# A sandwich of attention and routed experts on one core: the experts' matrices first copied into another layout in memory

## The chip, the cores and the metric

The kernel runs on one core of a Trainium2 chip. The metric is device time in microseconds, from the start of the program to its end; of several executions the median counts. The core has a matrix engine (PE, with its weight loads shown as PEld), a vector engine (DVE), a scalar engine (ACT), GpSimd (POOL) and a synchronisation engine (SP) that here issues transfers. ACT and POOL issue transfers too. All transfers are carried by the core's 16 DMA engines. Everything is float32 but for a few small masks.

## The reference

The input is x, 8 sequences of 512 rows of 256 numbers. Cut to what matters, the reference computes:

```python
x = x + layernorm(attention(layernorm(x)))     # 16 heads of 128 in 4 groups, causal, sinusoidal positions
x = x + layernorm(ffn(layernorm(x)))

def ffn(x):                                    # 4096 rows
    scores = softmax(x @ gate_w.T)             # 64 experts
    topk_w, topk_idx = top_k(scores, 6)
    # an expert takes the first 64 rows (CAP) that chose it, in the order of rows
    d = (silu(buf @ w_gate) * (buf @ w_up)) @ w_down   # per expert: 64 x 256, 256 x 176 twice, 176 x 256
    y = sum over the 6 choices of topk_w * d
    return y + (silu(x @ sh_gate.T) * (x @ sh_up.T)) @ sh_down.T     # shared expert, width 352
```

Every expert has three matrices: w_gate and w_up of 256 x 176 and w_down of 176 x 256, 180 KB each. The kernel takes the 64 experts two at a time, as 32 pairs; a pair's matrices are 1.08 MB.

## The kernel before, in words

The eight sequences are worked through one after the other, and each as 16 heads, so that one loop runs over 128 heads k. The order of the instructions on each engine is the order in which the program writes them: the whole loop stands under a manual schedule.

One step of the loop does parts of several heads. It writes the scores of head k in four row tiles (PE), adds the causal mask and finds each row's extreme (DVE, line 293), and takes the exponential (ACT, line 296). `weigh` (line 300) divides by the row sums: a reciprocal on DVE and four multiplications on POOL (line 306). The weights of head k - 1 must be turned before they can be multiplied with the values. `turned` (line 313) does this in two halves: DVE turns 32 x 32 blocks into the tile eb (line 322), SP writes eb to a memory tensor ex_d (line 326), waits for it, and reads it back in four transfers with the blocks at their new places, as et (line 329). `mix` of head k - 2 (line 343) multiplies et with the values on PE (pav, line 349), and ACT copies the result to ao (line 109). `project` of head k - 3 multiplies ao with the output matrix (po, line 361). So the exchange through memory that starts in one step is needed by PE in the next step.

Beside the heads stands other work, hung into the steps by tables: the keys and values of the next sequence, and for a sequence that is done its normalisation, its shared expert and its routing. After five sequences (EARLY) the rows of the experts are settled but for places left free. From head 94 on `experts` (line 621) is advanced at several places of each step: first tables, then the 32 pairs. Once it runs in full, a head's step advances it four times, which is two pairs.

A pair m passes through stages (lines 628 to 642). At its step m POOL gathers its 128 rows (gx, line 513). One step later ACT issues the loads of its gate and up matrices, `load_gate_up` (line 517): two transfers into the tile wgu, each with 2 x 128 rows of 1408 bytes, since a partition holds two neighbouring rows of an expert's matrix, and the two experts lie apart in memory. Two steps later PE turns the gathered rows (ptx), a step after that it multiplies them with gate and up (pgu, line 549), and ACT issues `load_down` (line 526): one transfer into wd, 2 x 88 rows of 2048 bytes. Then the hidden rows are turned (pth), and five steps after the gather PE multiplies them with wd (pd, line 575); ACT scales the result (dd, line 583), and POOL adds it into the memory tensor y_d by an indirect transfer (line 586). The tiles wgu and wd have two buffers each, so a load waits until PE is done with the pair two before it.

One more pair, "late", takes rows of the last three sequences. It is chosen at run time; its loads are issued by SP (table["m"] is a register), at head 102. A loop at the end would take further such pairs; it runs no turns here.

Transfers issued by SP and by ACT take eight completion semaphores in turn: each waits, on its issuing engine, for the transfer eight before it in the program's order. A transfer that waits holds up what stands behind it on that engine; on ACT these are exponentials and copies.

The memory tensors are tiles of a pool, made by dram.tile at the start of the kernel.

Of the kernel before, what the change touches and what calls it, by code (L numbers as in the profile page):

```python
# [11 lines left out]
F32 = mybir.dt.float32  # L12
# [7 lines left out]
P = 128  # L20
B, T, E = 8, 512, 256
# [7 lines left out]
NH = G * QPG  # L29
NX, F, TOPK, CAP = 64, 176, 6, 64  # L30
FC = F // 2
NM = NX // 2
# [12 lines left out]
def sandwich_kernel(ctx, tc, x, wq, bq_t, wkv, bk_t, bv, wo, gate_wt, w_gate, w_up, w_down,  # L45
                    sh_gate_t, sh_up_t, sh_down_t, pe_t, out):
    nc = tc.nc
# [3 lines left out]
    dram = ctx.enter_context(tc.tile_pool(name="dram", bufs=1, space=bass.MemoryType.DRAM))  # L51
# [10 lines left out]
    x1_d = dram.tile([NT, E], F32, tag="x1_d", name="x1_d")  # L62
    xg_d = dram.tile([ET_ROWS + 1, ROW], F32, tag="xg_d", name="xg_d")
    y_d = dram.tile([2 * (ET_ROWS + CAP), E], F32, tag="y_d", name="y_d")
    lxg_d = dram.tile([NT - ET_ROWS, LROW], F32, tag="lxg_d", name="lxg_d")
    ly_d = dram.tile([NT - ET_ROWS, E], F32, tag="ly_d", name="ly_d")

# [55 lines left out]
    with ExitStack() as part:  # L123
# [38 lines left out]
        for half, (t, w) in enumerate(((sg_sb, sh_gate_t), (su_sb, sh_up_t))):  # L162
            nc.sync.dma_start(out=t[:, :, :FSH], in_=w.rearrange("(c p) n -> p c n", p=P))
            nc.sync.dma_start(out=t[:, :, FSH:],
                              in_=gate_wt.rearrange("(c p) n -> p c n", p=P)[:, :, ts(half, NX // 2)])
# [39 lines left out]
        def zeros():  # L205
            zero = p1.tile([P, ROW], F32, tag="hid", name="zero")
            nc.gpsimd.memset(zero, 0.0)
            nc.sync.dma_start(out=xg_d[ET_ROWS : ET_ROWS + 1, :], in_=zero[0:1, :])
            nc.sync.dma_start(out=y_d[ET_ROWS : ET_ROWS + CAP, :], in_=zero[:CAP, :E])
            yield  # L210
            for r in range(ET_ROWS + CAP, 2 * (ET_ROWS + CAP), P):
                n = min(P, 2 * (ET_ROWS + CAP) - r)
                nc.sync.dma_start(out=y_d[r : r + n, :], in_=zero[:n, :E])
                yield
# [85 lines left out]
        def weigh(k):  # L300
            l = live[k]
            recip = small.tile([P, NI], F32, tag="recip", name=f"recip_{k}")
            nc.vector.reciprocal(recip, l["total"])  # L303
            engine = nc.gpsimd if k < NK - 1 else nc.vector
            for n, e in enumerate(l["e"]):
                engine.tensor_scalar(e, e, recip[:, n : n + 1], 1.0, ALU.mult, ALU.mult)  # L306
# [200 lines left out]
        table, pairs = {}, {}  # L507

        def start_pair(m):

            l = pairs[m] = {"m": m}
            l["gx"] = p3.tile([P, ROW], F32, tag="gx", name=f"gx_{m}", bufs=3)
            nc.gpsimd.indirect_dma_start(
                out=l["gx"], out_offset=None, in_=xg_d[:, :],
                in_offset=bass.IndirectOffsetOnAxis(ap=table["idx"][:, m, 0:1], axis=0))

        def load_gate_up(key):
            l, queue = pairs[key], nc.sync if key == "late" else nc.scalar
            m = l["m"]

            l["wgu"] = p3.tile([P, 2, 2, 2, F], F32, name=f"wgu_{key}", **l.get("wgu_at", {"tag": "wgu"}))
            for k, w in enumerate((w_gate, w_up)):
                queue.dma_start(out=l["wgu"][:, :, k, :, :].rearrange("p e c f -> p e (c f)"),
                                in_=w[ds(m * 2, 2)].rearrange("e (p c) f -> p e (c f)", p=P))

        def load_down(key):
            l, queue = pairs[key], nc.sync if key == "late" else nc.scalar
            m = l["m"]
            l["wd"] = p3.tile([FC, 2, 2, E], F32, name=f"wd_{key}", **l.get("wd_at", {"tag": "wd"}))
            queue.dma_start(out=l["wd"].rearrange("p e c h -> p e (c h)"),  # L530
                            in_=w_down[ds(m * 2, 2)].rearrange("e (p c) h -> p e (c h)", p=FC))

        def turn_rows(key):
            l = pairs[key]
            pt = ps_s.tile([P, 2, P], F32, tag="s", name=f"ptx_{key}")
            rows = l["gx"][:, :E].rearrange("s (p c) -> s c p", c=2)
            for c in range(2):
                nc.tensor.transpose(pt[:, c, :], rows[:, c, :], ident)
            l["gxt"] = p3.tile([P, 2, P], F32, tag="gxt", name=f"gxt_{key}")
            on_dve(l["gxt"], pt)  # L540
            l["gw"] = p3.tile([P, 2], F32, tag="gw", name=f"gw_{key}", bufs=4)
            nc.vector.tensor_copy(l["gw"], l["gx"][:, E + 2 * key : E + 2 * key + 2])
# [78 lines left out]
        def experts():  # L621


            yield from tables()
            yield
            yield from free_slots()
            yield
            for m in range(NM + 5):
                if m < NM:
                    start_pair(m)  # L630
                for behind_, step in ((5, down), (3, gate_up), (4, turn_hidden), (2, turn_rows),
                                      (1, load_gate_up), (3, load_down)):
                    if 0 <= m - behind_ < NM:
                        step(m - behind_)
                yield
                if 0 <= m - 3 < NM:
                    gate_up_hidden(m - 3)
                if 0 <= m - 5 < NM:
                    scatter(m - 5)
                if m == NM + 4:  # L640
                    pairs["all"] = True
                yield
# [288 lines left out]
        queries(0)  # L931
        assert len(units) == 12
        behind, ahead = {}, iter(())
        routed, zeroing = experts(), zeros()
        twice, finishing = False, False
        FIRST_FREE = (EARLY + 1) * NH + 6

        def side(s, place):
            behind.pop(f"{s}{place}", lambda: None)()
            if not b:  # L940
                for u in rest.get(f"{s}{place}", ()):
                    u()

        for k in range(NK):
            b, s = divmod(k, NH)
            active = k >= EARLY * NH + 14
            scores(k, 0)
            scores(k, 1)
            if 0 <= k - 1 < NK - 2:
                turned(k - 1)  # L950
            if twice and not finishing:
                next(routed, None)
            scores(k, 2)
            scores(k, 3)
            if k == NK - 1:
                turned_at_once(k - 1)
            weigh(k)
            side(s, "A")
            if k >= 3:
                project(k - 3)  # L960
            side(s, "B")
            if active:
                next(routed, None)
            if s == (9 if b == EARLY + 1 else 8):
                next(ahead, lambda: None)()
            if k + 1 < NK:
                queries(k + 1)
            side(s, "M")
            if k >= 2:
                mix(k - 2)  # L970
            if active and not finishing:
                next(routed, None)
            if not b:
                next(zeroing, None)
                next(zeroing, None)
            if k == FIRST_FREE:

                work = table["work"]
                table["rest"] = nc.values_load(work[0:1, 0:1], min_val=0, max_val=NM - 1)
                table["m"] = nc.values_load(work[0:1, 1:2], (ET.DVE, ET.SP), min_val=0, max_val=NM - 1)  # L980
                pairs["late"] = {"m": table["m"], "wgu_at": {"tag": "wgu_late", "bufs": 1},
                                 "wd_at": {"tag": "wd_late", "bufs": 1}}
                load_gate_up("late")
                load_down("late")
            if s == 2 and b:
                behind = feed_forward(b - 1)
            side(s, "D")
            if s == 6 and b + 1 < B:
                ahead = prepare(b + 1)

            for _ in range((0, 0, 0, 0, 0, 0, 1, 0, 1, 1, 2, 1, 1, 1, 2, 1)[s] if b == EARLY + 1 else
                           (0, 0, 0, 0, 0, 0, 1, 1, 1, 1, 1, 1, 1, 1, 2, 1)[s]):
                next(ahead, lambda: None)()
            twice = active and k > EARLY * NH + NH
            if twice and not finishing:
                next(routed, None)

            if finishing and s in (12, 14):
                next(routed, None)
            if active and not finishing and "all" in pairs:  # L1000
                routed, finishing = finish_early(), True
# [11 lines left out]
        with tc.For_i(0, table["rest"], 1) as n:  # L1013
            m = nc.values_load(table["work"][0:1, ds(n + 2, 1)], (ET.DVE, ET.SP), min_val=0, max_val=NM - 1)
# [4 lines left out]
            for b in range(EARLY, B):  # L1019
                q, tag = [(p1, "hid"), (p2, "v"), (p2, "v")][b - EARLY]  # L1020
                xg = q.tile([P, NI, LROW], F32, tag=tag, name=f"rest_xg_{b}")
                nc.sync.dma_start(out=xg, in_=rows_of(lxg_d, b * T - ET_ROWS))
                q, tag = [(p1, "y"), (p2, "x"), (p2, "x")][b - EARLY]
# [68 lines left out]
```

## Time and profile before

Three runs took 1455.51, 1459.09 and 1459.84 us; the median is 1459.09 us.

| | |
|---|---|
| profiled execution, its own time | 1456.37 us |
| its span | 1454.6 us |
| PE busy | 1403.1 us, 96% |
| DVE, ACT, POOL busy | 892.8, 505.8, 429.2 us |
| moved by DMA | 252.03 MB in 160790 packets, mean 173 GB/s |
| ACT's queue (q10) | 28672 packets, 39.85 MB, 9.9% of 16 engines' span |
| SP's queue (q1) | 125869 packets, 201.52 MB, 46.5% |
| loads of wgu, first and last issue | 980.8 and 1247.2 us |
| loads of wd, first and last issue | 995.5 and 1260.5 us |

The page gives one execution, taken by the hardware profiler. An engine's busy time is the sum of its instructions; what it spends on issuing transfers is not counted as busy. The page shows the span in 40 equal slices of 36.4 us, where a digit is a busy share in tenths, and PEclk is the granted clock of PE in tenths of full speed. In a list of waits, "A <- B: 8.3, 4, 4.3" says that A stood idle until B for 8.3 us in all, 4 times, 4.3 at the longest. In a list in order of time, each line has start, duration, engine, line of the program, operation, and in brackets the idle time before it and what ended it. A transfer is shown at its issue; where its data landed is seen in the packet records of the trace.

### The profile page before, as it was taken

Reading aid. Unit: us, or ns where it says so; the run is one execution under the profiler, and the core shown is the slowest. Engines: PE = TensorE matmul, PEld = TensorE weight load, DVE = VectorE, ACT = ScalarE, POOL = GpSimd, SP = SyncE. Lnnn points to the kernel's source line nnn. Section 1 sums busy time; section 2 is a strip of 40 time slices with the busy share of each in tenths; the row PEclk is TensorE's granted clock in tenths of the full one; section 3 lists DMA queues with packets and bytes.
Section 4 is the critical chain, followed back from the end, with each engine's and each line's share of the span. In section 5 each row is a group of like instructions: output and inputs, shape, how many; then the busy total and the mean of one; then the engine's idle time right before and its main releaser. Section 6 shows DMA issues by size and latency. Waiting matters only on the chain. (4 is left out here: it accounts for less than half of the span.)

```text
span 1454.6 us, 18553 instructions
## 1 busy us (share of the span) xinstructions
PE 1403.1 (96%) x5310; PEld 855.2 (59%) x5310; DVE 892.8 (61%) x3097; ACT 505.8 (35%) x1442; POOL 429.2 (30%) x686
## 2 busy tenths in 40 slices
PE   9999999999999999999999999999989999999895
PEld 5665665656556665666566665655545655556563
DVE  5565576656765577557665676576455454567634
ACT  2333343234422333234323442233433243434431
POOL 2222232123211231124211321125434444344511
PEclk9999999999999999999999999999999999999998
DMA  7664464355544554445534554449999889878812
GB/s 258 195 201 141 144 181 146 95 156 167 164 128 128 163 174 128 122 145 182 155 109 139 165 173 128 123 139 264 258 261 234 230 241 260 220 196 235 248 53 81
DMA packets 160790, 252.03 MB, mean 173 GB/s; under 512 B 16412, under 2 KB 136189, under 8 KB 160685
## 3 DMA queue, kind: packets, MB, share of 16 engines
q1 hardware_dynamic: 125869, 201.52, 46.5%
q10 hardware_dynamic: 28672, 39.85, 9.9%
q0 software_dynamic: 6144, 9.44, 3.4%
q8 instruction: 44, 0.72, 0.2%
q14 instruction: 61, 0.50, 0.1%
HBM read 143.01 MB, written 107.74 MB: 172 GB/s over the span
## 5 line engine op out<-in xcount | busy, mean ns | idle before, releaser
L306 POOL TENSOR_SCALAR e<-e,recip 128x128 f32<-128x128 f32 x508 | 274.1, 597 | 787.0 <-DVE recip L303 749.1
L296 ACT ACTIVATE e<-e,least 128x128 f32<-128x128 f32 (+3 forms) x512 | 285.8, 559 | 377.5 <-DVE least L293 338.9
L289 PE MATMUL psc<-kt,qt 128*128 128x128 f32 (+3 forms) x1024 | 310.0, 442 | 13.9 <-DVE qt L279 6.7
L349 PE MATMUL pav<-et,v 128*128 128x512 f32 (+3 forms) x1024 | 300.0, 436 | 5.0 <-DMA et<-ex_d 3.4
L349 PEld LDWEIGHTS pav<-et,v 128*128 128x128 f32 x1024 | 194.9, 192 | 166.8 <-issue 122.6
L293 DVE CUSTOM_DVE_ANT_0 e<-psc,mask 128x128 f32<-128x128 f32 (+3 forms) x512 | 232.7, 479 | 74.9 <-PE psc L289 67.5
L361 PE MATMUL po<-wo_sb,ao 128*128 128x256 f32 x1024 | 243.5, 381 | 0.7 <-ACT ao L109 0.7
L276 PE MATMUL pq<-xnt,wq_sb 128*128 128x512 f32 x512 | 242.1, 595 | 0.0
L361 PEld LDWEIGHTS po<-wo_sb,ao 128*128 128x128 f32 x1024 | 193.0, 190 | 72.3 <-issue 40.7
L322 DVE STREAM_TRANSPOSE eb<-e 128x128 f32<-128x128 f32 x756 | 228.1, 365 | 8.6 <-DMA ex_d<-eb 6.4
L109 ACT COPY ao<-pav 128x512 f32<-128x512 f32 x128 | 74.9, 585 | 427.4 <-PE pav L349 406.7
L289 PEld LDWEIGHTS psc<-kt,qt 128*128 128x128 f32 x1024 | 167.9, 192 | 90.7 <-issue 22.2
L279 DVE SCALAR_TENSOR_TENSOR qt<-pq,bq_sb,pe_sb 128x512 f32<-128x512 f32 x128 | 95.5, 746 | 93.5 <-PE pq L276 93.3
L276 PEld LDWEIGHTS pq<-xnt,wq_sb 128*128 128x128 f32 x512 | 96.3, 191 | 69.7 <-issue 64.2
L303 DVE RECIPROCAL recip<-total 128x4 f32<-128x4 f32 x128 | 22.8, 178 | 121.6 <-ACT e L296 120.6
L296 ACT ACTIVATION_READ_ACCUMULATOR e<-e,least 128x1 f32 x512 | 95.8, 187 | 0.0
L586 POOL DMA_INDIRECT y_d<-dd,idx x32 | 51.2, 1600 | 130.3 <-DMA y_d<-dd,idx 85.6
L248 PE MATMUL pk<-xnt,wkv_sb 128*128 128x512 f32 x128 | 60.3, 594 | 0.2 <-ACT xnt L109 0.2
L261 DVE TENSOR_TENSOR v<-pv,bv_sb 128x512 f32<-128x512 f32 x32 | 22.1, 691 | 60.8 <-PE pv L259 60.8
L259 PE MATMUL pv<-wkv_sb,xnt 128*128 128x512 f32 x128 | 59.1, 593 | 0.0
L112 DVE COPY ht<-pth 88x256 f32<-88x256 f32 x32 | 13.4, 418 | 67.8 <-PE pth L566 52.9
L251 DVE SCALAR_TENSOR_TENSOR kt<-pk,bk_sb,pe_sb 128x512 f32<-128x512 f32 x32 | 24.0, 750 | 47.4 <-PE pk L248 47.4
(197 smaller groups left out, 1118.2 us busy)
## 6 DMA issues: line engine op xcount, KB each, us to landing
ex_d<-eb SPq DMA_DIRECT2D x126, 640.0 KB
et<-ex_d SPq DMA_DIRECT2D x504, 160.0 KB
wgu<-in_w_gate ACTq DMA_DIRECT2D x32, 352.0 KB
wgu<-in_w_up ACTq DMA_DIRECT2D x32, 352.0 KB
wd<-in_w_down ACTq DMA_DIRECT2D x32, 352.0 KB
y<-y_d ACTq DMA_DIRECT2D x10, 512.0 KB
x<-in_x SPq DMA_DIRECT2D x8, 512.0 KB
x_d<-x SPq DMA_DIRECT2D x8, 512.0 KB
```

The lines of the kernel that those rows point to most:

```text
L109: nc.scalar.copy(dst, src)
L248: nc.tensor.matmul(pk, lhsT=wkv_sb[:, c, g, 0, :], rhs=s["xnt"][:, c, :], start=c == 0, stop=c == NC - 1)
L259: nc.tensor.matmul(pv, lhsT=s["xnt"][:, c, ts(i, P)], rhs=wkv_sb[:, c, :, 1, :], start=c == 0, stop=c == NC - 1)
L276: nc.tensor.matmul(pq, lhsT=wq_sb[h // QPG][:, c, ts(h % QPG, D)], rhs=seqs[b]["xnt"][:, c, :], start=c == 0, stop=c == NC - 1)
L279: nc.vector.scalar_tensor_tensor(qt, pq, bq_sb[:, h : h + 1], pe_sb, ALU.add, ALU.add)
L289: nc.tensor.matmul(psc[:, :w], lhsT=l["qt"][:, ts(i, P)], rhs=seqs[b]["kt"][h // QPG][:, :w], start=True, stop=True)
L293: nc.vector.tensor_tensor_reduce(out=e, in0=psc[:, :w], in1=mask[:, T - w :], scale=-1.0 / math.sqrt(D), scalar=BIG, op0=ALU.add, op1=ALU. ...
L296: nc.scalar.activation(e, e, AF.Exp, bias=l["least"][:, i : i + 1], scale=-1.0, accum_out=l["total"][:, i : i + 1])
L306: engine.tensor_scalar(e, e, recip[:, n : n + 1], 1.0, ALU.mult, ALU.mult)
L322: nc.vector.transpose(blocks.rearrange("p c j t -> p j c t"), l["e"][i][:, js[0] * P : (js[-1] + 1) * P].rearrange("p (j c t) -> p j c t", ...
L349: nc.tensor.matmul(pav[:, :, j:, :], lhsT=seqs[b]["v"][:, j, ts(g, D)], rhs=l["et"][:, :, AT[j] : AT[j] + NI - j, :], start=j == 0, stop=j ...
L361: nc.tensor.matmul(po[b][i // 2][:, i % 2, :], lhsT=ao[:, ts(i, P)], rhs=wo_sb[:, h, :], start=h == 0 and i % 2 == 0, stop=h == NH - 1, sk ...
```

## The change

Two memory tensors are added, wgu_d and wd_d, which hold the matrices of the 32 pairs once more. In wgu_d a partition's part of a pair lies side by side: two experts by gate and up by two rows, 5632 bytes. In wd_d it is two experts by two rows of the down matrix, 4096 bytes.

`repack` fills them by 96 transfers from memory to memory, three for each pair, issued on ACT's queue. The loop advances it after `weigh` from head 8 on: twice where k is a multiple of 4, else once, so that it is done at head 84. The pairs' loads then read the new tensors: one transfer for gate and up together, 128 rows of 5632 bytes, and one for down, 88 rows of 4096 bytes. The late pair reads the matrices where they were, as before.

```diff
+    wgu_d = dram.tile([NM, P, 2, 2, 2 * F], F32, tag="wgu_d", name="wgu_d")
+    wd_d = dram.tile([NM, FC, 2, 2 * E], F32, tag="wd_d", name="wd_d")
...
         def load_gate_up(key):
-            l, queue = pairs[key], nc.sync if key == "late" else nc.scalar
+            l = pairs[key]
             m = l["m"]
 
             l["wgu"] = p3.tile([P, 2, 2, 2, F], F32, name=f"wgu_{key}", **l.get("wgu_at", {"tag": "wgu"}))
+            if key != "late":
+                nc.scalar.dma_start(out=l["wgu"].rearrange("p e k c f -> p (e k c f)"),
+                                    in_=wgu_d[m].rearrange("p e k f -> p (e k f)"))
+                return
             for k, w in enumerate((w_gate, w_up)):
-                queue.dma_start(out=l["wgu"][:, :, k, :, :].rearrange("p e c f -> p e (c f)"),
+                nc.sync.dma_start(out=l["wgu"][:, :, k, :, :].rearrange("p e c f -> p e (c f)"),
                                 in_=w[ds(m * 2, 2)].rearrange("e (p c) f -> p e (c f)", p=P))
 
         def load_down(key):
-            l, queue = pairs[key], nc.sync if key == "late" else nc.scalar
+            l = pairs[key]
             m = l["m"]
             l["wd"] = p3.tile([FC, 2, 2, E], F32, name=f"wd_{key}", **l.get("wd_at", {"tag": "wd"}))
-            queue.dma_start(out=l["wd"].rearrange("p e c h -> p e (c h)"),
+            if key != "late":
+                nc.scalar.dma_start(out=l["wd"].rearrange("p e c h -> p (e c h)"), in_=wd_d[m].rearrange("p e h -> p (e h)"))
+                return
+            nc.sync.dma_start(out=l["wd"].rearrange("p e c h -> p e (c h)"),
                             in_=w_down[ds(m * 2, 2)].rearrange("e (p c) h -> p e (c h)", p=FC))
+
+        def repack():
+
+            for m in range(NM):
+                for k, w in enumerate((w_gate, w_up)):
+                    nc.scalar.dma_start(out=wgu_d[m, :, :, k, :],
+                                        in_=w[ts(m, 2)].rearrange("e (p c) f -> p e (c f)", p=P))
+                    yield
+                nc.scalar.dma_start(out=wd_d[m], in_=w_down[ts(m, 2)].rearrange("e (p c) h -> p e (c h)", p=FC))
+                yield
...
-        routed, zeroing = experts(), zeros()
+        routed, zeroing, repacking = experts(), zeros(), repack()
...
             weigh(k)
+            if k >= NH // 2:
+                for _ in range(1 + (k % 4 == 0)):
+                    next(repacking, None)
             side(s, "A")
```

## The prediction

> **What bounds the kernel now.** I read the page first, then busy times by stage, then PE's waits, then single heads. The page's busy line and its slices of the span:
>
> ```profile
> PE 1403.1 (96%) x5310; PEld 855.2 (59%) x5310; DVE 892.8 (61%) x3097; ACT 505.8 (35%) x1442; POOL 429.2 (30%) x686
> PE   9999999999999999999999999999989999999895
> PEclk9999999999999999999999999999999999999998
> DMA  7664464355544554445534554449999889878812
> ```
>
> PE is busy nearly everywhere; the DMA engines are half busy through the heads and full in one stretch, slices 27 to 31, where the 32 expert pairs run. Busy times by stage (PE, PEld, DVE, ACT, POOL, then granted clock, DMA share, GB/s) of a stretch of plain heads, of the pairs' stage, and of its two worst 10 us:
>
> ```profile
> 500.00:600.00 100.00, 98.47 (x350) 60.75 (x349) 68.98 (x240) 37.09 (x109) 26.73 (x47) 1.00 0.49 149
> 980.00:1270.00 290.00, 276.49 (x1290) 160.09 (x1289) 156.78 (x547) 102.16 (x280) 125.68 (x143) 0.98 0.95 246
> 1060.00:1070.00 10.00, 5.72 (x23) 3.10 (x22) 4.44 (x16) 4.83 (x19) 2.31 (x2) 0.66 0.97 238
> 1230.00:1240.00 10.00, 7.05 (x31) 3.74 (x30) 2.07 (x7) 2.80 (x7) 4.71 (x6) 0.86 0.99 242
> ```
>
> In the pairs' stage PE idles 290 - 276.5 = 13.5 us, and where it stood longest it then ran at a granted clock of 0.66 and 0.86. PE's waits on DMA, over the whole span, and one of them in order of time:
>
> ```profile
> PE pd L575 <- DMA wd<-in_w_down: 8.3, 4, 4.3
> PE pav L349 <- DMA et<-ex_d: 3.4, 1, 3.4
> ...
> 1060.44 0.41 ACTq L523 DMA_DIRECT2D wgu<-in_w_up  x1
> 1061.98 0.32 ACTq L530 DMA_DIRECT2D wd<-in_w_down  x1
> 1064.55 1.97 PE L575 MATMUL pd<-wd,ht 88*64 88x256 f32 x8 [4.28 <-DMA wd<-in_w_down]
> ```
>
> The down product waits for its matrix. By the packet records of the trace that matrix was issued at 1051.96, its first packet moved 7.0 us later, behind the gate and up rows in the same queue, and it landed at 1063.4. The 3.4 us wait stands at 1374, outside this stage.
>
> **The change, part by part.**
>
> *Added: 96 copies from memory to memory.* repack issues 3 per pair on ACT's queue, after weigh, from head 8 to head 84: two in every fourth head, one in the others. A gate or up copy is 256 rows of 1408 B, a down copy 176 of 2048 B, 0.36 MB each. (a) ACT's issues: 374 to 482 ns each for the like loads, so 96 x 0.43 = 41 us of ACT, which is 33% busy there. In a plain head ACT has finished its exponentials at 504.25 and waits until 507.28 for PE before it copies ao; two issues of 0.43 fit these 3 us, so I cost them at nothing; without that cover, 41 us of ACT would delay ao and the next exponentials. (b) Every hardware DMA also waits for the one that used its semaphore before, eight DMAs back; with six or seven a head that is a transfer issued about a head ago, so I cost it at nothing for ACT and for SP. (c) The DMA engines. They are 49% busy, so there is room on average; the question is the exchange's deadline:
>
> ```profile
> 502.30 0.34 SPq L326 DMA_DIRECT2D ex_d<-eb  x1
> 505.33 1.73 SPq L329 DMA_DIRECT2D et<-ex_d  x4
> 513.04 2.32 PE L349 MATMUL pav<-et,v 128*128 128x512 f32 x8
> ```
>
> The last packet of these four loads ended 4.0 us after 505.33, 3.7 before the mix that reads them. Over heads 8 to 84 this slack is 2.6 to 3.4 us in plain heads, 4 to 13 in those with feed-forward work. Ten heads with two copies have a tight successor: mean slack 3.0, less 0.4 from last packet to release (as the 2.59 us write and the issue of et at 3.03 us show): 2.6. The copies go out about 1 us before et and share the engines with it; et needs 2.2 us of engine time in a 2.6 us window. So two copies of c us delay et by 2c - 1.3, and PE waits 10 x (2c - 3.9) us in all, from c = 1.95 up.
>
> No row of before copies memory to memory. Below: a 1408 B load row takes 60 ns undisturbed (median), 256 x 60 / 16 = 0.96 us, cost 0. Above: if reading and writing memory don't overlap, a row takes the load's 60 plus a store's (5120 B to memory take 196, so 54 for 1408 B), with the 1.3 that contention adds to a load row in the pairs' stage (78 against 60): 148 ns, c = 2.4, cost 10 x 0.9 = 9 us; the down copy (176 rows of 84 ns, 0.92 us) is of the same size. A row of a copy does both, read memory and write it, so it is nearer to the upper row, which is built of both; I take three quarters of the way, c = 2.05 and **+1.5 us**, keeping 0 and 9, and 20 (c = 2.95) for a fifth more than the upper row.
>
> A page speaks against the copies: the Trainium skill, "DMA: Bandwidth & Descriptors", section "Latency and other measured facts", gives copies between HBM tensors about 207 to 214 GB/s at best. An estimate by that page is 0.36 MB / 0.21 = 1.7 us a copy, where the load's row gives 0.96; the formula above would then cost nothing, with little to spare. No run here shows it yet.
>
> *Removed and replaced: the pairs' loads.* Of 96 DMAs on ACT's queue 64 remain; 32 issues of 0.43 = 14 us less on ACT in 290 us. Packets: 512 of 1408 B a pair become 128 of 5632, 176 of 2048 B become 88 of 4096. Packet records of the stage: 1408 B mean 78 ns, 2048 B mean 130; 5120 B mean 204 on SP's queue. So before, (16384 x 78 + 5632 x 130) / 16 = 125 us per engine. After, 5632 B by the 5120 row 225 ns, 4096 B as 163: (4096 x 225 + 2816 x 163) / 16 = 86 us. Saved: 39 of 275 us of engine time, so the share falls from 0.95 to about 0.81 with the bytes unchanged. The first packet of wd then moves a few us earlier, since the gate and up rows ahead of it take 128 x 225 / 16 = 1.8 us alone for a pair where they took 512 x 78 / 16 = 2.5, and every other transfer meets emptier engines.
>
> What that is worth. At most: the four pd waits (0.81 + 4.28 + 0.29 + 2.95 = 8.3), the wait of pav at 1050 (1.3), and the slow clock after the two long ones, 5.72 x 0.34 + 7.05 x 0.14 = 2.9; sum 12.5. With the gap at 987, where the first rows are turned (2.5), and the clock of 0.90 and 0.93 around it (1.7), 16.7. At least: 0, if another wait comes last at the same places; at 1060 DVE too had waited 3.6 us for ex_d, and ACT 7.2. I take two thirds of 12.5, **-8 us**, since at the two long waits wd landed 1.1 and 1.9 us before pd began, so that an earlier landing moves pd until another wait comes last. Next late is then ex_d or the scatter into y_d, for which POOL waits 85.6 us: both use the same engines and gain too.
>
> The late pair and the heads after 98 keep their instructions: 0. The order of PE, DVE, POOL and SP instructions is unchanged but for line numbers.
>
> **Sum.** -8 + 1.5 = -6.5 us. The profiled execution took 1456.4 us (span 1454.6 and 1.8 around it), so 1449.9; it lies 2.7 under the median of 1459.09, so against that median 1452.6. I say **1452 us**. About 0.3%, 4.4 us, is what a measurement of this kernel can tell from no change.
>
> **Rivals.** *The engines stay full* (nothing measurable). The exchange, gathers and scatters remain, 0.81 is a mean, and the waits may only change names. For it: SP waited 115 us for ex_d in this stage, and ex_d is not touched. Against: the four longest pd waits are on the very transfer that shrinks. Also in this case: the long rows are cut again in the queue, so that packets stay as they were (against: 5120 B rows show as whole packets), or the gain and a copy cost of 4 to 9 cancel. Time: 1455 to 1463.
>
> *The copies make et late* (slower). One mechanism: memory-to-memory rows so slow that et misses its mix in the ten tight heads. It decides from 10 x (2c - 3.9) = 8, c = 2.35 us a copy; measurably slower from c = 2.6. For it: that is only 2.7 times the load's price and 1.1 times the upper row with both streams. Against: a plain head has 4 us of free engine time. At c = 3: 21 - 8 = +13, 1472.
>
> **How the numbers follow.** Forecast (gain of 4.4 or more) 0.50; engines stay full or all cancels 0.25; copies make et late 0.25. Faster 0.50, same 0.25, slower 0.25. The low end is the larger sum without copy cost: 1459 - 16.7 = 1442. The high end reaches into the slower case, c = 2.85: 18 - 8 = +10, 1469, with some 0.1 above. The forecast's own range is 1442 to 1455.
>
> **What would show it.** Right: pd's wait for wd under 2 us in all, the stage from 980 to 1270 shorter by 5 to 10 us with a DMA share of 0.80 to 0.87, no granted clock of 0.66 there; 1408 B rows on ACT's queue only as copies; PE's wait on et below 3 us in heads 8 to 84. Wrong: PE waiting "pav <- DMA et" at every fourth head (copy price), pd's gaps unchanged with wd now read from wd_d (engines full), or ACT waiting on a DMA semaphore ahead of ao between 100 and 950 us (b).

## The result, and the profile after

Over 14 runs each, the changed kernel took a median of 1458.89 us (1453.91 to 1463.06) and the kernel before 1459.69 us (1455.51 to 1462.57). The ratio is 0.9997, with a 95% interval of 0.9985 to 1.001: no difference, to within 2 us. The forecast had been 1452 us.

The profiled execution of the changed kernel took 1459.99 us, with a span of 1458.3. Its page, in the lines that answer to those shown of before: PE's busy time, the slices of the span, and the total of packets.

```profile
PE 1403.0 (96%) x5310; PEld 853.8 (59%) x5310; DVE 893.3 (61%) x3097; ACT 508.1 (35%) x1442; POOL 431.1 (30%) x686
PE   9999999999999999999999999999989999999895
DMA  7676675477755775567655754458999889778812
DMA packets 168566, 286.64 MB, mean 197 GB/s; under 512 B 17276, under 2 KB 137053, under 8 KB 168461
```

PE's row is the same digit for digit. The DMA row is fuller in the slices of the copies, with 34.6 MB more moved, and almost as full as before in the pairs' stage. The busy times of that stage (PE, PEld, DVE, ACT, POOL, granted clock, DMA share, GB/s), to be held against 276.49 us of PE and a share of 0.95 before:

```profile
980.00:1270.00 290.00, 276.94 (x1291) 159.71 (x1289) 155.17 (x543) 103.37 (x280) 125.09 (x143) 0.98 0.91 246
```

PE idles 13.1 us there instead of 13.5, and the DMA share fell by 0.04 where 0.14 was forecast. What PE waits for, over the whole span:

```profile
PE pav L352 <- DMA et<-ex_d: 5.5, 1, 5.5
PE pgu L569 <- DVE hid L579: 4.9, 1, 4.9
PE ptx L558 <- DMA gx<-xg_d,idx: 4.5, 2, 3.3
...
PE pd L595 <- DMA wd<-wd_d: 1.3, 2, 1.0
```

The wait for the down matrices has indeed gone from 8.3 to 1.3 us. In its place stand a wait of 4.9 us on the hidden rows and 4.5 us on the gathered rows; 3.3 of the latter are at 988, where the first rows are turned and PE had stood 2.5 us before. (The 5.5 is at 1378, near the end of the heads, where 3.4 stood before.) The wait on the hidden rows is at the same place as the longest wait of before, and the list in order of time shows what lies behind it:

```profile
1050.92 0.35 SPq L329 DMA_DIRECT2D ex_d<-eb  x1
...
1065.70 0.34 ACTq L538 DMA_DIRECT2D wd<-wd_d  x1
1065.73 1.87 SPq L332 DMA_DIRECT2D et<-ex_d  x4
1065.77 1.81 DVE L325 STREAM_TRANSPOSE eb<-e 128x128 f32<-128x128 f32 x6 [6.81 <-DMA ex_d<-eb]
1066.14 0.40 ACT L299 ACTIVATE e<-e,least 128x128 f32<-128x128 f32 x1 [8.88 <-DMA wgu<-wgu_d]
...
1068.23 2.62 PE L569 MATMUL pgu<-wgu,gxt 128*64 128x352 f32 x8 [4.91 <-DVE hid L579]
```

The write of eb to ex_d was issued at 1050.92 and the reads of et, which wait for it, at 1065.73: 14.8 us for a transfer that takes 2.6 us in a plain head. By the packet records its first packet moved 4.5 us after the issue, when the late pair's down matrix and the next x, issued ahead of it on SP's queue, were still moving, and its last one 9.7 us after that. DVE cannot overwrite eb until then; ACT is held behind a transfer whose semaphore is not free; the hidden rows come late, and PE with them. In the kernel before the same write took 11.2 us there, and DVE had waited 3.6 us for it. This reads the pd wait of before as the last name in a row of several waits, not as the cause; the run with the late pair later, below, bears on it.

The copies themselves, as the instructions that touch wgu_d and, in the last line, wd_d (durations in ns, least, median, most, of the issue on ACT):

```profile
L547 ACTq DMA_DIRECT2D wgu_d<-in_w_gate x32: 569/580/688, 85.4 to 815.2; - x32
L547 ACTq DMA_DIRECT2D wgu_d<-in_w_up x32: 548/549/863, 86.1 to 823.0; - x32
L526 ACTq DMA_DIRECT2D wgu<-wgu_d x32: 325/327/366, 981.6 to 1245.7; - x32
...
L550 ACTq DMA_DIRECT2D wd_d<-in_w_down x32: 838/844/1379, 94.5 to 831.2; - x32
```

An issue costs 0.55 to 0.58 us in the median, and 0.84 for the down copies, where 0.43 was taken; still no PE gap over 0.6 us lies between 80 and 970 us. By the packet records a copied row of 1408 bytes takes 60 ns in the median and 79 in the mean, as a load's row does.

### The profile page after: what moved, and what is told of

Its sections match the earlier page's. It is cut to its first block, busy times and chain, and to the rows that moved or that the text cites. A ratio compares the mean times of both kernels' runs of the same rounds, so it can differ in the third digit from the quotient of the medians.

```text
span 1458.3 us, 18552 instructions
## 1 busy us (share of the span) xinstructions
PE 1403.0 (96%) x5310; PEld 853.8 (59%) x5310; DVE 893.3 (61%) x3097; ACT 508.1 (35%) x1442; POOL 431.1 (30%) x686
```

## The experiments

Two theories stood against each other. A: the long rows give several microseconds and the copies take them back. B: neither does anything. The later runs ask what the pairs' loads do cost, and in what: rows, issues or bytes. Ratios are to the kernel before, with 95% intervals; a ratio is turned into microseconds with 1459.

### The copies alone

```diff
-            if key != "late":
-                nc.scalar.dma_start(out=l["wgu"]..., in_=wgu_d[m]...)
-                return
+            queue = nc.sync if key == "late" else nc.scalar
             for k, w in enumerate((w_gate, w_up)):
-                nc.sync.dma_start(
+                queue.dma_start(
...                                          (load_down likewise; repack stays)
```

> The 96 copies are made as in the changed kernel, but the pairs' loads read the matrices where they were, in rows of 1408 and 2048 bytes. Theory A (the long rows give 4 to 8 us, and the copies take them back): slower than before by 4 to 8 us. Theory B (neither does anything: the copies lie in free engine time, and the long rows relieve no wait that comes last): within 2 us of before, no PE wait for et between heads 8 and 84, copy rows of 1408 bytes at a median of 60 ns.

Measured: 1.0004 (0.9991 to 1.0018), +0.6 us. No PE wait for et stands in heads 8 to 84; the one of 4.0 us is at 1374. The copies cost nothing that these runs can tell. By the packet records the copy rows of 1408 bytes took 60 ns in the median, as expected, and 76 in the mean.

### The long rows alone

```diff
+            if key != "late":
+                rows = w_gate[ds(min(m * 2, NX - 4), 4)].rearrange("e r f -> (e r f)").rearrange("(p n) -> p n", p=P)
+                nc.scalar.dma_start(out=l["wgu"].rearrange("p e k c f -> p (e k c f)"), in_=rows)
+                return
...                                          (load_down likewise: two experts' w_down as 88 rows)
```

> No copies; the pairs' loads read 128 rows of 5632 bytes and 88 of 4096 straight from the experts' matrices as they lie in memory. This leaves out the right placing of the numbers: the products are of other numbers of the same matrices. Theory A: faster than before by 4 to 8 us. Theory B: within 2 us of before; the packets of 5632 bytes take a mean of 260 to 280 ns as in the changed kernel, since what a packet takes here is mostly waiting for other transfers, not work.

Measured: 0.9991 (0.9977 to 1.0005), -1.3 us. The pairs' stage of this kernel:

```profile
980.00:1270.00 290.00, 277.15 (x1293) 159.44 (x1292) 158.12 (x545) 104.41 (x284) 125.27 (x143) 0.98 0.91 247
```

PE's busy time and the DMA share are those of the changed kernel, without any copy. The 5632-byte packets took a mean of 264 ns, as expected, but "mostly waiting" is too strong: their median is 215 ns, so about a fifth of the mean is waiting. Theory A falls: there was no gain of 4 to 8 us for the copies to take back. A gain of some 1 to 3 us is not excluded.

### No loads, an eighth, a half, three quarters

```diff
+            if key != "late" and m >= 2:
+                l["wgu"] = kept["wgu", m % 2]
+                return
-            l["wgu"] = p3.tile([P, 2, 2, 2, F], F32, ...)
+            l["wgu"] = kept["wgu", key] = p3.tile([P, 2, 2, 2, F], F32, ...)
...                                          (load_down likewise)
```

> Only the first two pairs' matrices are loaded; pairs 2 to 31 multiply with these again, so 30 of 32 loads of 1.08 MB are left out and those pairs' results are of the wrong experts. This bounds what any change of the pairs' loads can give. Theory A (the stage hangs on the loads): faster by 9 to 16 us, with PE idle under 4 us between 980 and 1270. Theory B in its strong form (the exchange, the late pair's loads and the gathers hold the stage up by themselves): faster by under 4 us.

Measured: 0.9877 (0.9853 to 0.9901), -18.0 us, somewhat more than theory A's 9 to 16, with PE idle for 3.4 us. The three that follow keep every issue, every row and every wait, and shorten the rows.

```diff
+                for k, w in enumerate((w_gate, w_up)):
+                    queue.dma_start(out=l["wgu"][:, :, k, 0, : F // 4],
+                                    in_=w[ds(m * 2, 2)].rearrange("e (p c) f -> p e (c f)", p=P)[:, :, : F // 4])
...                                          (F // 4 of 2 * F: an eighth; F: a half; 3 * F // 2: three quarters; load_down likewise)
```

> The kernel before, where the loads of pairs 2 to 31 keep their number, rows, waits and places but move an eighth of each row (176 and 256 bytes), so that seven eighths of those matrices are left out and the products are of other numbers. If bytes are what the loads cost: nearly as fast as without the loads, 13 to 18 us faster than before. If rows or issues and their waits are what they cost: less than 6 us faster.

> The same with half of each row (704 and 1024 bytes); half of the matrices is left out. If the cost is in proportion to bytes: 8 to 9 us faster than before. If it sets in only near full engines, as queues do: 12 to 16 us faster, most of what leaving the loads out gives.

> As with half of each row, but three quarters (1056 and 1536 bytes): a quarter of the matrices of pairs 2 to 31 is left out. Half of the bytes gave all of the 18 us that leaving the loads out gave, so the cost sets in between half and all. Threshold theory: DMA share about 0.86 from 980 to 1270, faster than before by 9 to 15 us. If the cost begins right at half and grows evenly: 9 us. If it is still flat at three quarters: 16 to 18 us.

Measured, with the DMA share and PE's idle time between 980 and 1270 us (290 less PE's busy time there):

| moved of pairs 2 to 31 | ratio | us | DMA share | PE idle, us |
|---|---|---|---|---|
| all (the kernel before) | 1 | 0 | 0.95 | 13.5 |
| three quarters | 0.9885 (0.9864 to 0.9906) | -16.8 | 0.88 | 4.3 |
| a half | 0.9875 (0.9855 to 0.9894) | -18.2 | 0.77 | 4.0 |
| an eighth | 0.9874 (0.9853 to 0.9895) | -18.4 | 0.63 | 4.7 |
| nothing | 0.9877 (0.9853 to 0.9901) | -18.0 | 0.56 | 3.4 |

The pairs' stage with nothing and with three quarters moved:

```profile
980.00:1270.00 290.00, 286.62 (x1348) 167.24 (x1347) 169.35 (x592) 110.78 (x300) 140.64 (x161) 1.00 0.56 145
```

```profile
980.00:1270.00 290.00, 285.75 (x1337) 165.85 (x1336) 168.43 (x583) 108.19 (x295) 139.42 (x160) 0.99 0.88 226
```

The faster kernels finish the pairs 10 to 14 us before 1270, so the end of this window holds other work there; up to its own last down product, three quarters has a share of 0.89.

So the loads do cost 18 us, and what costs is bytes: with an eighth of them, but all rows, issues and semaphore waits, the cost is gone. And it is the last quarter that costs nearly all. Of the cases expected for three quarters, the result lies in "still flat"; its interval, 14 to 20 us, reaches into the 9 to 15 of the threshold theory. The DMA share does not tell this by itself: the changed kernel and the long rows alone stand at 0.91, close to the 0.88 of three quarters, and took as long as before, since they still move all the bytes (246 and 247 GB/s against 226). A share is a sum of packets' durations, and these contain waiting. Fewer bytes also make each burst of loads shorter; whether the fullness of the stage or the length of a burst decides, these runs do not separate.

### Each copy twice

```diff
+                    for again in range(2):
-                    nc.scalar.dma_start(out=wgu_d[m, :, :, k, :], ...)
+                        nc.scalar.dma_start(out=(wgu_d, wgu2_d)[again][m, :, :, k, :], ...)
...                                          (wd_d likewise; two further memory tensors)
```

> As the changed kernel, but each copy is issued twice, into two places: two copies in a head and four in every fourth. By the prediction's formula with the measured row (60 to 79 ns, c = 1.0 to 1.25 us): et is delayed by 4c - 1.3 = 2.7 to 3.7 us in ten heads with 2.6 us of slack, so 1 to 11 us slower than the changed kernel. If the copies only fill idle time and et is served beside them: within 2 us of the changed kernel.

Measured: 1.0091 (1.0067 to 1.0115), +13.3 us. PE's longest wait by name, and two entries in order of time:

```profile
PE pav L354 <- DMA et<-ex_d: 18.9, 14, 3.4
```

```profile
500.11 2.39 PE L354 MATMUL pav<-et,v 128*128 128x512 f32 x8 [1.67 <-DMA et<-ex_d]
...
509.36 1.99 PE L354 MATMUL pav<-et,v 128*128 128x512 f32 x5 [1.25 <-DMA et<-ex_d]
```

One of the 14 waits is the 3.4 us near the end that the other kernels have too, and two, 1.9 us together, come after the last copy, at 1086 and 1261. The other eleven, 13.6 us, lie between 97 and 825 us. Ten of them, 12.3 us, stand in the steps 9, 17, 21, 33, 37, 49, 53, 65, 69 and 81 of the loop, each the step after one with four copies. By the packet records these are the ten steps after one with two copies in the changed kernel whose slack, from et's last packet to the mix, was 2.6 to 3.3 us before, 3.0 in the mean; the others after a doubled one had 4.8 or more. The eleventh wait stands in step 50. In the changed kernel the slack of the ten is 1.5 us in the mean and 0.95 at the least. So the exchange has a cliff, the prediction put it at the right heads, and the changed kernel stands before it.

With c = 1.3 us (256 rows of 79 ns on 16 engines) the formula delays et by 2 x 1.3 - 1.3 = 1.3 us with two copies, where the slack fell by 1.5, and gives 10 x (4 x 1.3 - 3.9) = 13 us with four, where the ten waits make 12.3. That the second meets so well is partly luck: by this kernel's own mean row, 71 ns, it would be 6 us. The time lies above the 1 to 11 us that were expected.

### The late pair later, and the first loads earlier

```diff
+            if k == FIRST_FREE + 2:
                 load_gate_up("late")
+            if k == FIRST_FREE + 3:
                 load_down("late")
```

> The kernel before, with the late pair's loads issued at heads 104 and 105 in place of 102, away from the load of the next x. If the gap of some 4 us near 1060, named pd <- wd before and pgu <- hid after the change, comes from ex_d standing behind these loads and x in SP's queue: no PE gap over 2 us between 1050 and 1075, and faster by 4 to 7 us. If it comes from the pairs' own loads: same within 2 us, with the gap still there.

Measured: 0.9992 (0.9975 to 1.0008), -1.2 us. The long gap did go: between 1045 and 1075 there remain 0.8 and 1.6 us, where 1.3 and 4.3 stood. But the time did not fall by 4, and the pd wait of 2.8 us near 1231 is still there. PE's longest waits for pd in this run, to be held against 8.3 us, 4 times, before:

```profile
PE pd L575 <- DMA wd<-in_w_down: 4.3, 3, 2.8
```

So neither case came as expected. The reading of the gap is supported: it went although the pairs' own loads were not touched. Its price was expected too high. The profiled execution, 1451.8 us, was among the fastest of its twelve, whose median is 1456.5; why the median fell by so little is not shown.

```diff
+            for m in range(2):
+                pairs[m] = {"m": m}
+                load_gate_up(m)
+                load_down(m)
             yield from tables()
...                                          (the pairs' loop then leaves the loads of pairs 0 and 1 out)
```

> The kernel before, with the loads of pairs 0 and 1 issued at head 94, about 30 us earlier, while the engines are half idle. If the gap of 2 to 3 us near 987 (the first rows turned) is the gather waiting beside these loads: that gap falls under 1.5 us and the time by 2 to 5 us. If DVE's order makes it: the gap stays, same within 2 us.

Measured: 0.9983 (0.9967 to 0.9999), -2.5 us. The gap near 987 is gone, and the time fell as expected. A new PE wait of 2.0 us stands at 955, for which the profile names no releaser. The six transfers at once at head 94 did hold et up: its last packet ended 11.3 us after the first issue, where a plain head takes 4.0. But it ended 1.8 us before PE went on, so that et made this wait is likely and not shown.

### The two moves together, without and with the new layout

```diff
+            if k in (86, 90):
+                m = (k - 86) // 4
+                pairs[m] = {"m": m}
+                load_gate_up(m)
+                load_down(m)
             side(s, "A")
...                                          (and the late pair's loads at heads 104 and 105)
```

> The kernel before with the late pair's loads at heads 104 and 105, and the loads of pairs 0 and 1 at heads 86 and 90, where the exchange has 7 to 13 us of slack. It takes 2.2 of 34.6 MB of loads out of the full stretch and one burst away from another. By the single runs (1.2 and 2.5 us, the second with a new PE gap of 2.0 at 955 that the earlier heads avoid): faster than before by 3 to 7 us.

> The changed kernel with the same two moves. If the layout gives nothing, as the long rows alone did: within 2 us of the two moves without it. If the long rows help once the bursts are apart: 3 us or more faster than these.

Measured: without the layout 1450.96 us, 0.995 (0.9931 to 0.9968), -7.3 us; with it 1448.62 us, 0.993 (0.991 to 0.9949), -10.2 us. Both beat the kernel before, and so the changed one, which took the same time. The layout's part, 2.3 us by the medians, lies between the two cases expected, and the intervals overlap, so whether it adds something here stays open. The two moves without it keep a DMA share of 0.93 in the pairs' stage and still give 7 us: it is not the mean share alone that counts.

These two kernels also load pair 0's gate and up in the same stretch of half-idle engines, at 847 us, once in short and once in long rows, and so price the rows side by side. By the packet records 512 rows of 1408 bytes took 70 ns in the mean, 2.24 us of each engine; 128 rows of 5632 bytes took 289 ns, 2.32 us. The second pair's loads gave 2.21 and 2.30. So in the mean a long row of gate and up costs what its four short ones cost; by the medians, 215 against 4 x 60 = 240 ns, it costs a tenth less. The down matrices of the first pair took 1.73 us in rows of 2048 bytes and 1.37 in rows of 4096, those of the second 1.60 and 1.62.

## Why the prediction was wrong

**What bounds the kernel: right in its stage, wrong in its cause.** The pairs' stage does hold some 18 us that the loads cause. The prediction's largest sum was 16.7 us; leaving the loads out gave 18.0.

**(a) ACT's issues and (b) the semaphores: right.** The issues took longer than taken (0.55 to 0.84 us against 0.43), and the cover held: ACT's wait for pav between 80 and 860 us is 265.9 us after and 263.9 before; the issues lie inside it. SP waited there for transfers of the copies for some 8 us in all, 0.9 at the longest, and PE lost nothing by it.

**(c) The copies' price: too high, with no harm.** +1.5 us was taken, by c = 2.05, for which the prediction's own formula gives 2.0; c is 1.3 and the cost 0.6 us, inside the noise. Of the bounds the lower one, the load's row, was the nearer: by the packet records a copied row takes the 60 ns of a loaded one in the median, so writing memory adds nothing there to reading it. The slack was read as 2.6 to 3.4 us in plain heads; the steps 8, 18, 36 and 50 had only 0.7 to 1.3 us, but none of them follows two copies.

An estimate of 1.7 us a copy stands in the prediction, by the Trainium skill ("DMA: Bandwidth & Descriptors", section "Latency and other measured facts"), whose figure is for rows of 16 KiB. A gate or up copy here takes near that from its first packet to its last beside the exchange: 1.9 us in the median (3.25 less 1.37 after the issue).

**The step that failed** is "Saved: 39 of 275 us of engine time". It priced the old rows by their mean in the full stage (78 and 130 ns) and the new ones by a 5120-byte row on SP's queue (204 ns). Those rows are all stores of eb into ex_d, not loads, and they were hardly disturbed: 200 ns in the mean among the heads, 204 in the full stage. In that stage the new rows took 274 and 243 ns: (4096 x 274 + 2816 x 243) / 16 = 113 us instead of 86, so 13 saved. Even those 13 are not all work, since a packet's duration there contains its waiting for others. By rows with little waiting, 60 and 84 ns for the short ones and 215 and 159 for the long ones (medians, and for the down matrices' rows the lower quartile), it is 91 against 83 us: 8 saved, of 275. The bytes stayed, and in the runs with fewer bytes it was these that cost.

**"Two thirds of 12.5, -8 us"** failed with it. The pd waits did go, and others came last in their place. The prediction named that as its lower end and put 0.25 on "the engines stay full", which is what happened; the argument it gave against, that the longest waits lie on the very transfer that shrinks, took the last-named of several waits for the cause. Its larger sum also has a slip: the clock of 0.90 and 0.93 costs 1.4 us when taken by PE's busy time as its other clock term is, not 1.7.

**The rival "the copies make et late"** did not come true, but its mechanism did at twice the copies, in ten heads, as it had counted.

## What to carry to other kernels

Before paying for a layout that makes rows longer, price both shapes in the same direction and in the same stretch of the trace, and once more in a quiet one: a packet's time under contention is not all work that can be saved. Where DMA engines are near full, ask first what an experiment with fewer bytes gives; here a quarter fewer gave 17 us, and rows two and four times as long about nothing. Then take bytes or bursts out of the full stretch, into one with idle engines and known slack.

## What was not expected of the hardware

Leaving out the loads took 18.8 us off the profiled span (1454.6 to 1435.8), and 8.0 of them are PE's busy time for the same instructions:

```profile
PE 1395.1 (97%) x5310; PEld 851.1 (59%) x5310; DVE 892.9 (62%) x3097; ACT 507.5 (35%) x1442; POOL 431.4 (30%) x686
```

The granted clock of the run is 0.994 there and 0.987 before. In the clock records of the kernel before, the clock falls to 0.5 for 3.4 or 6.8 us at each of the five PE gaps of 2.1 to 4.3 us between 980 and 1400 us, and at none of the shorter ones. So a long gap there costs its own length and then a stretch at a low clock. It is not so every time: with the two moves PE stood 2.9 us at 1062, and with each copy twice 3.4 us at 1388, and the clock stayed at 1.00. With each copy twice there are also fourteen gaps of 0.8 to 1.7 us between 90 and 830 us, and the clock up to 980 us stayed at 1.00 (the column before the DMA share):

```profile
0.00:980.00 980.00, 956.15 (x3343) 584.87 (x3344) 612.61 (x2108) 331.99 (x969) 237.31 (x447) 1.00 0.71 222
```

The cost of the pairs' loads is not in proportion to their bytes: the first three quarters cost 1 us, the last quarter 17.
